# A graph layer on one core: the running maximum written to SBUF, and other shares of the gathers

## The chip, the core and the metric

The kernel runs on one core of a Trainium2 chip. The core has five engines, each with a queue of its own that it works through in order: TensorE (PE; its loads of weights are shown as PEld), VectorE (DVE), ScalarE (ACT), GpSimd (POOL), and SyncE (SP), which here only issues DMAs. They meet at semaphores. SBUF is the working memory of 128 partitions, PSUM the memory of eight banks into which PE writes.

The metric is the time on the device in microseconds, as the median of several runs. A profile is one execution with every instruction recorded.

## The reference

A graph of 12500 nodes and 200000 edges, sorted by destination, goes through a two-layer network; features have 128 elements in fp32. Cut to what matters:

```python
h    = maximum(layernorm(x), 0)
w    = edge_weight / segment_sum(edge_weight, dst)[dst]
feat = relu(h @ W_pool + b_pool)
neigh = segment_max(feat[src] * w, dst)          # layer 1
rst  = h @ W1_self + neigh @ W1_neigh + b1
h    = relu(rst / norm(rst))
neigh2 = segment_sum(h[src] * w, dst) / deg      # layer 2
out  = x + relu(h @ W2_self + neigh2 @ W2_neigh + b2)
```

Each layer fetches one row of 128 features for every edge, by the edge's source, and reduces the rows of the edges that share a destination: by maximum in layer 1, by sum in layer 2. `edge_attr_128` is not used.

## The kernel before

**Tiling.** Edges are taken in groups of G = 512 consecutive ones, 391 groups (the last has 320). A group is four chunks of 128 edges, one edge to a partition. Both layers are one loop over the groups, written out as a software pipeline under `manual_schedule`: what iteration i issues belongs to groups i, i-1, i-2 and so on, and each engine's order is the order in the text.

**Fetching.** A chunk's rows come from a table in HBM (`feat_d`, `h_d`) by an indirect DMA that POOL issues (`gather`, L520), 128 rows each. Some chunks come another way: the node features also lie transposed in SBUF (`one_way`, `other_way`: features by nodes), and VectorE or ACT copies the column of each edge's source out of it (class `Columns`, functions `two_by_two`, L800, two columns an instruction, and `one_by_one`, L788, one an instruction). The column addresses are loaded into registers sixteen at a time from a list in SBUF (`places_of`, L742), which SP loads (`load`, L738), two iterations ahead of the first fetch. `every` says how often an engine takes over a chunk: in layer 1 VectorE takes chunk 1 of each sixth group from group 32 and ACT chunk 3 of each 5.5th; in layer 2 VectorE takes chunk 1 of each third group and ACT chunk 2 of each 3.5th. The fetches of one chunk, eight of sixteen columns, are spread over the iterations before its group; the fetched chunk lies features by edges, so PE must turn it (layer 1 multiplies it by `W_pool`, `multiplied`, L951, and ACT writes it back, `cut`, L954; layer 2 transposes it into the PSUM tile `flip`, `turned`, L1151, and ACT writes it back, `back`).

**Buffers for the rows.** `ring` holds the gathered groups: 18 at first, later 14, and 8 from about group 113 on and in all of layer 2. A gather waits until the group that had its buffer has been used.

**Layer 1, by iteration.** ACT weights the four chunks of group i by the edge weights into `gs` (L1035). PE turns group i-1 into the PSUM tile `pm` (L1040), features by edges. VectorE runs a scan over the 512 edges of group i-2 (L1055): state = max(kept + state, new), where `kept` (`kt`, from `keep_d`) is 0 inside a destination and about -3e38 at its first edge; the scan overwrites `pm` in place, and its last column is the next group's start (`carry`, L1074). No two destinations end within one pair of edges, so 256 values are kept: VectorE copies the odd elements from `pm` to `sc` (L1078), and overwrites an element with its even neighbour where the mask says that a new destination begins at the odd one (`copy_predicated`, L1081). PE turns `sc` back (L1095), ACT copies it to SBUF (L1050), PE multiplies it by a selection matrix built by VectorE (`pick`, L1067; L1104), and ACT writes the 48 columns of the window into the transposed neighbour sums (L985). Whenever the groups of a node tile are done, the node steps (`nodes1`: L851 to L890) run, spread over six iterations; they store the rows of h to `h_d`. `side_step` does background jobs on the edge lists (`edges1` to `fitness`) for layer 2 in between, until 1599 us.

`kt` is loaded by SP for KEPT = 4 groups at a time (`keep_rows`, L602), into one of two buffers, at the start of each fourth iteration.

The first 16 groups (FIRST) go another way: their rows of x are gathered and normalised before the table exists, and the products of rows and weights are made on VectorE (L1084), with the weights in a `gs` tile.

**Layer 2, by iteration.** VectorE makes the weighted places of group i (L1165, L1169), with a fetch between the two; PE multiplies rows and places of group i-1 into a PSUM tile `pa` (`window_product`, L1175, L1177; three buffers); VectorE adds the `pa` of group i-2 to the window of the transposed sums (`window_add`, L1180), after another fetch. The node steps (`nodes2`) run as in layer 1, from iteration 60 on. Three first groups (`early_groups`), gathered before all of `h_d` is written, are put right and added in between.

Of the kernel before, what the change touches and what calls it, by code (L numbers as in the profile page):

```python
# [18 lines left out]
P = 128  # L19
# [22 lines left out]
TABLES_AT = (16512, 66880)  # L42
BURST = 16
HIGH = 1.0e30
KEPT = 4
PAIR = 2


# [1 line left out]
def gnn_kernel(ctx, tc, x, src, dst, ew, w_pool, b_pool, w1s, w1n, b1, w2s, w2n, b2, out):  # L50
# [871 lines left out]
    with tc.manual_schedule(), tc.tile_pool(name="ew", bufs=3) as wk, \  # L922
# [13 lines left out]
        products = {}  # L936
        bycol = []
        for k, engine, copy, j, every, first in (
                (0, mybir.EngineType.DVE, two_by_two, 1, 6, FIRST + 16),
                (1, mybir.EngineType.Activation, one_by_one, 3, 5.5, FIRST + 12)):  # L940

            def rows_of_chunk(g, j=j):
                return buffer(g, True)[:, j, :]

            def slot(g, k=k, rows_of_chunk=rows_of_chunk):
                return rows_of_chunk(g) if k else picked[:, bycol[0].place[g], :]

            def multiplied(g, _, k=k, slot=slot):
                product = products[g, k] = ps.tile([P, D], F32, name="pn")
                nc.tensor.matmul(product, (ones_r if k else minus_plus)[0:3, :P], bias_kept[0:3, :], start=True, stop=False)  # L950
                nc.tensor.matmul(product, slot(g), W["pool"], start=False, stop=True)  # L951

            def cut(g, _, k=k, rows_of_chunk=rows_of_chunk):
                nc.scalar.activation(rows_of_chunk(g), products.pop((g, k)), AF.Relu,  # L954
                                     **({} if k else {"scale": signs}))
# [7 lines left out]
        def keep_tile():  # L963
            return wk.tile([P, KEPT, G], BF16, name="kt", bufs=2)

# [36 lines left out]
        for i in range(max(turn) + 6):  # L1002
# [6 lines left out]
            if i >= NG:  # L1009
                window_copy(due(5))  # L1010
            node_stage(5)
            if i % KEPT == 0 and i and i + 2 < NG:
                keep_rows(i + 2, keep_tile())
            if FIRST <= i < NG:
                gts[i] = gather(buffer(i, True), feat_d, i, besides=bycol)

            if i < FIRST:
                pms[i] = ps.tile([P, G], F32, name="pm", bufs=2)
                if i > 0:
                    nc.scalar.activation(pms[i], raws.pop(i).rearrange("p q n -> p (q n)"), AF.Relu, bias=bp_col)  # L1020
                if i + 1 < FIRST:
                    weight_rows(i + 1, wk.tile([P, G], F32, name="gs", bufs=2))
                    raw_columns(pn, i + 1)
                if i + 2 < FIRST:
                    raw_scale(i + 2)
                    raw_norm(i + 2)
                if i + 1 < FIRST:
                    raw_back(i + 1)

            elif i < NG:  # L1030
                t, r, ne, chunks = edges_of(i)
                gss[i] = wk.tile([P, G], F32, name="gs", bufs=2).rearrange("p (q d) -> p q d", d=D)
                gt = gts.pop(i)
                for j, k in reversed(chunks):
                    nc.scalar.activation(gss[i][:k, j, :], gt[:k, j, :], AF.Copy, scale=ewT[:k, t, j, r:r + 1])  # L1035
            if FIRST < i <= NG:
                gs = gss.pop(i - 1)
                pms[i - 1] = ps.tile([P, G], F32, name="pm", bufs=2)
                for j, k in edges_of(i - 1)[3]:
                    nc.tensor.transpose(pms[i - 1][:, j * P:j * P + k], gs[:k, j, :], ident[:k, :k])  # L1040
# [11 lines left out]
            if g is not None:  # L1052
                ne = edges_of(g)[2]
                kt, pm = kts.pop(g), pms.pop(g)
                nc.vector.tensor_tensor_scan(pm[:, :ne], kt[:, :ne], pm[:, :ne], carry,  # L1055
                                             op0=OP.add, op1=OP.max)
                bycol[0].ahead()
            picks = []
# [12 lines left out]
            if g is not None:  # L1071
                if g + 1 < NG:
                    carry = wk.tile([P, 1], F32, name="carry")
                    nc.vector.tensor_copy(carry, pm[:, ne - 1:ne])  # L1074
                sc = scs[g] = wk.tile([P, G // 2], F32, name="sc", bufs=2)
                two = pm[:, :ne].rearrange("p (c two) -> p c two", two=2)
                new = kt[:, :ne].bitcast(I16).rearrange("p (c two) -> p c two", two=2)
                nc.vector.tensor_copy(sc[:, :ne // 2], two[:, :, 1])  # L1078
            pick()
            if g is not None:  # L1080
                nc.vector.copy_predicated(sc[:, :ne // 2], new[:, :, 1], two[:, :, 0])  # L1081
            if i < FIRST:
                rows = gts.pop(i).rearrange("p q n -> p (q n)")
                nc.vector.tensor_tensor(pms[i], pms[i] if i else rows, ws.pop(i), OP.mult)  # L1084
            node_stage(1)
            node_stage(3)
            node_stage(4)
# [34 lines left out]
                c.turn(i, c.load, c.fetch)  # L1122
            for c in bycol:
                c.turn(i, c.multiplied)
        assert not busy
        i = NG
        side_step()
# [4 lines left out]
    with tc.manual_schedule(), tc.tile_pool(name="ew2", bufs=3) as wk, \  # L1132
            tc.tile_pool(name="ep2", bufs=2, space=PSUM) as ps:
        place = ps.tile([P, 2 * Q, CW], F32, bufs=1)
        hit, iota = place[:, :Q, :], place[:, Q:, :]
        flip = ps.tile([P, 2, P], F32, bufs=1)
        for j in range(Q):
            nc.vector.tensor_copy(iota[:, j, :], cols[:, 0, SHIFT[j]:SHIFT[j] + CW])
        nothing = wk.tile([P, LW], BF16, bufs=1)
# [2 lines left out]
        bycol = []  # L1142
        for k, engine, copy, j, every, first in (
                (0, mybir.EngineType.DVE, two_by_two, 1, 3, 17),
                (1, mybir.EngineType.Activation, one_by_one, 2, 3.5, 12)):

            def slot(g, j=j):
                return buffer(g, False)[:, j, :]

            def turned(g, _, k=k, slot=slot):  # L1150
                nc.tensor.transpose(flip[:, k], slot(g), ident)  # L1151

            def back(g, _, k=k, slot=slot):
                by_scalar(slot(g), flip[:, k], **({} if k else {"scale": signs}))

            bycol.append(Columns(engine, copy, None, other_way, 1, lists_of(k), slot,
                                 ((-2, turned), (0, back)), 3, j, every, first, NG - 1))
            bycol[k].turned, bycol[k].back = turned, back
# [57 lines left out]
        for i in range(max(turn) + 2):  # L1216
# [22 lines left out]
                next(first_groups, None)  # L1239
            if i == NG - 1:  # L1240
                for n in (HI - 2, HI - 1):
                    own[n] = flip[:, 0] if n % 2 else ps.tile([P, Q, D], F32, name="pl", bufs=1)[:, 0]
                    linear_own(own[n], n, "2s")
            by_two, by_one = bycol
            by_two.fetch_one(i)
# [133 lines left out]
```

## Time and profile before

| | us |
|---|---|
| time, median of 3 runs | 3544.11 (3543.92 to 3545.5) |
| the profiled execution's own time | 3545.64 |
| its span, from first to last instruction | 3543.9 |
| DVE busy | 3130.4 (88%) |
| ACT busy | 3081.4 (87%) |
| POOL busy | 2619.8 (74%) |
| PE busy | 2211.6 (62%) |

Layer 1's gathers of `feat_d` end at 1838.4 us; those of `h_d` for the first groups follow. The page gives busy times by engine; groups of instructions by source line, with the mean time of one and the idle time in front of them, by what ended it; the waits list who waited for whom; the timeline lists instructions with start and length; and the windows give busy times and counts of a stretch of time. "issue" is idle time for which the profile shows no wait; loads of registers fall under it, as they are not counted as busy.

### The profile page before, as it was taken

To read this page: it belongs to the slowest core of one execution; us is meant where nothing else is said; L and a number is where in the kernel's file an instruction comes from. 1 tells how busy PE (TensorE), PEld (TensorE's weight loads), DVE (VectorE), ACT (ScalarE), POOL (GpSimd) and SP (SyncE) were. 2 spreads that over 40 slices of the span, in tenths; PEclk is the share of its full clock that TensorE was granted. 3 is DMA by queue.
4 is the path that set the end of the run, shared out by engine and by line. 5 is a ranking of instruction groups with operands and counts; after the bars stand their busy time and mean duration, and the time that the engine had idled before them with its cause. 6 is when DMAs were issued, how large, how long until landed. Compare 5 with 4: busy or idle time off the path is not lost.

```text
span 3543.9 us, 71968 instructions
## 1 busy us (share of the span) xinstructions
PE 2211.6 (62%) x9504; PEld 1920.0 (54%) x9504; DVE 3130.4 (88%) x16737; ACT 3081.4 (87%) x25633; POOL 2619.8 (74%) x2784
## 2 busy tenths in 40 slices
PE   7666666666666666566565667565565556556556
PEld 6455555555656555555554555555455555455545
DVE  7799999999999999998866888888888888888887
ACT  6689999999999999898967888888888888888885
POOL 6577777777777777777777777777777777777774
PEclk8665555555555555555555555555555555555555
DMA  6433332333333333332222222222222222222221
GB/s 223 130 97 90 94 88 83 88 86 88 86 87 86 88 86 88 86 88 86 83 82 54 54 60 75 60 63 63 60 60 63 63 60 62 63 59 59 62 62 49
DMA packets 132987, 280.13 MB, mean 79 GB/s; under 512 B 49446, under 2 KB 58764, under 8 KB 132494
## 3 DMA queue, kind: packets, MB, share of 16 engines
q0 software_dynamic: 88544, 181.42, 20.2%
q1 hardware_dynamic: 43214, 93.11, 7.8%
q14 instruction: 414, 3.39, 0.3%
q8 instruction: 79, 1.29, 0.2%
q10 hardware_dynamic: 736, 0.92, 0.1%
HBM read 253.41 MB, written 21.87 MB: 78 GB/s over the span
## 4 chain that ended last, share of the span: by engine, by line
DVE 49%; ACT 16%; issue 12%; POOL 6%; PE 6%; DVEq 5%; DMA 4%; ACTq 1%; POOLq 0%
DVE gt L800 25%; ACT gt L788 7%; POOL gt L520 6%; DVE pm L1055 6%; DVE picked L800 5%; DVEq L742 5%; ACT gs L1035 4%; DMA gt<-feat_d,srcT 3%; PE pa L1177 2%; DVE sel L1067 2%; DVE s L1169 2%; PE pf L625 2%; DVE sc L1078 2%; DVE place L1165 1%; ACT rows L1050 1%
## 5 line engine op out<-in xcount | busy, mean ns | idle before, releaser
L788 ACT ACTIVATE gt<-way 128x1 f32 x21376 | 2125.3, 189 | 226.8 <-PE pa L1177 164.5
L520 POOL DMA_INDIRECT gt<-h_d,srcT x1318 | 1246.1, 945 | 411.5 <-issue 340.8
L520 POOL DMA_INDIRECT gt<-feat_d,srcT x1192 | 1127.5, 946 | 369.2 <-issue 302.0
L800 DVE SCALAR_TENSOR_TENSOR gt<-b,way 128x2 f32<-128x2 f32 x8000 | 1155.1, 215 | 182.7 <-issue 154.3
L1177 PE MATMUL pa<-s,gt 128*128 128x24 f32 x3102 | 736.5, 390 | 535.0 <-DVE s L1169 462.4
L1177 PEld LDWEIGHTS pa<-s,gt 128*128 128x128 f32 x3102 | 690.6, 327 | 573.4 <-DVE s L1169 502.8
L1040 PE MATMUL pm<-ident,gs 128*128 128x128 f32 x1499 | 393.5, 415 | 257.9 <-ACT gs L1035 232.1
L800 DVE SCALAR_TENSOR_TENSOR picked<-b,way 128x2 f32<-128x2 f32 x3840 | 541.7, 211 | 1.9 <-issue 1.7
L1055 DVE TENSOR_TENSOR_SCAN pm<-kt,carry,pm 128x512 f32<-128x512 bf16 x389 | 496.3, 1276 | 46.0 <-PE pm L1040 45.8
L1035 ACT ACTIVATE gs<-gt,ewT 128x128 f32<-128x128 f32 x1303 | 414.9, 390 | 73.6 <-DMA gt<-feat_d,srcT 60.1
L1104 PEld LDWEIGHTS pn<-sel,rows 128*128 128x128 f32 x1564 | 354.3, 313 | 170.5 <-ACT way L985 73.2
L1040 PEld LDWEIGHTS pm<-ident,gs 128*128 128x128 f32 x1499 | 283.9, 221 | 294.3 <-ACT gs L1035 276.6
L1104 PE MATMUL pn<-sel,rows 128*128 128x48 f32 x1564 | 356.9, 374 | 135.1 <-ACT way L985 58.6
L1067 DVE TENSOR_SCALAR sel<-cols,lastT,invT 128x48 f32<-128x48 f32 x782 | 245.7, 314 | 0.0
L1095 PE MATMUL pr<-ident,sc 128*128 128x128 f32 x782 | 235.9, 403 | 3.4 <-DVE r_first L291 2.4
L1081 DVE COPY_PREDICATED sc<-kt,pm 128x256 f32<-128x256 int16 x389 | 167.1, 430 | 0.0
L1095 PEld LDWEIGHTS pr<-ident,sc 128*128 128x128 f32 x782 | 164.5, 220 | 4.2 <-ACT gs L1035 3.7
L1078 DVE COPY sc<-pm 128x256 f32<-128x256 f32 x391 | 159.7, 408 | 3.8 <-PE pr L1095 3.7
L1050 ACT ACTIVATE rows<-pr 128x256 f32<-128x256 f32 x392 | 142.1, 363 | 5.3 <-PE pn L1104 5.2
L851 PE MATMUL pn<-w_2n,way 128*128 128x128 f32 x192 | 79.2, 515 | 102.2 <-DVE way L1180 102.2
L1165 DVE TENSOR_TENSOR place<-place,locT 128x96 f32<-128x96 f32 x391 | 100.8, 258 | 46.1 <-DVE way L1180 32.2
L520 POOL DMA_INDIRECT w2T<-feat_d,srcT x96 | 90.8, 946 | 51.9 <-issue 24.1
(303 smaller groups left out, 2735.1 us busy)
## 6 DMA issues: line engine op xcount, KB each, us to landing
kt<-keep_d SPq DMA_DIRECT2D x97, 512.0 KB
gt<-h_d,srcT POOLq DMA_INDIRECT x1318
gt<-feat_d,srcT POOLq DMA_INDIRECT x1192
feat_d<-fr SPq DMA_DIRECT2D x24, 256.0 KB
xr<-in_x SPq DMA_DIRECT2D x24, 256.0 KB
out<-o SPq DMA_DIRECT2D x24, 256.0 KB
h_d<-h SPq DMA_DIRECT2D x47, 128.0 KB
listed<-at_d SPq DMA_DIRECT2D x359, 0.5 KB
```

The costliest lines, as they stand in the source:

```text
L520: nc.gpsimd.indirect_dma_start(out=gt[:k, j, :], out_offset=None, in_=table_d[:, :], in_offset=bass.IndirectOffsetOnAxis(ap=srcT[:k, t, j, ...
L788: nc.scalar.activation(out, in_, AF.Copy, **scale)
L800: nc.vector.scalar_tensor_tensor(slot[:, r + e:r + e + 2], zero_high, columns_read[e], columns_read[e + 1].to_broadcast([P, 2]), op0=OP.su ...
L1035: nc.scalar.activation(gss[i][:k, j, :], gt[:k, j, :], AF.Copy, scale=ewT[:k, t, j, r:r + 1])
L1040: nc.tensor.transpose(pms[i - 1][:, j * P:j * P + k], gs[:k, j, :], ident[:k, :k])
L1050: nc.scalar.activation(rws[g][:k, j, :], pr[:k, j, :], AF.Copy)
L1055: nc.vector.tensor_tensor_scan(pm[:, :ne], kt[:, :ne], pm[:, :ne], carry, op0=OP.add, op1=OP.max)
L1067: nc.vector.tensor_scalar(part, cols[:k, 1, :], lastT[:k, t, j, r:r + 1], invT[:k, t, j, r:r + 1], op0=OP.is_equal, op1=OP.mult)
L1078: nc.vector.tensor_copy(sc[:, :ne // 2], two[:, :, 1])
L1095: nc.tensor.transpose(prs[g][:k, j, :], sc[:, j * P:j * P + k], ident)
L1104: nc.tensor.matmul(pas[g], rows[:k, j, :], sel[:k, j, :], start=j == 0, stop=j == len(chunks) - 1)
L1177: nc.tensor.matmul(pas[g][:, SHIFT[j]:SHIFT[j] + CW], gt[:k, j, :], s[:k, j, :], start=False, stop=j == 0)
```

## The change

In layer 1:

- The scan of a group from 16 on writes its result not into `pm` but into the group's weighted rows `gs` in SBUF, which PE has read by then. `carry` is read from there. The copy of the odd elements into `sc` is gone for these groups: `copy_predicated` changes the odd elements in place, reading the even ones from the same tile, and PE turns the odd elements, every second word, out of that tile. `gs` has four buffers, `sc` is gone; the first 16 groups put their copy into a `gs` tile.
- VectorE takes over chunk 1 of each 5.5th group, where it was each sixth.
- `kt` is loaded for three groups at a time, and at the end of the iteration, after the list loads.
- For the first 16 groups the product of rows and weights comes ahead of the copy.

In layer 2:

- The turned tiles lie in two PSUM tiles of a bank each, where they shared one; PE turns a chunk (`turned`) ahead of ACT's fetch and of the copies back in the order of the text. For the bank, `pa` has two buffers, where it had three.
- ACT takes over chunk 2 of each 3.25th group, where it was each 3.5th.

```diff
-KEPT = 4
+KEPT = 3
...
-                (0, mybir.EngineType.DVE, two_by_two, 1, 6, FIRST + 16),
+                (0, mybir.EngineType.DVE, two_by_two, 1, 5.5, FIRST + 16),
...
-            if i % KEPT == 0 and i and i + 2 < NG:
-                keep_rows(i + 2, keep_tile())
...
-                gss[i] = wk.tile([P, G], F32, name="gs", bufs=2).rearrange("p (q d) -> p q d", d=D)
+                gss[i] = wk.tile([P, G], F32, name="gs", bufs=4).rearrange("p (q d) -> p q d", d=D)
...
-                gs = gss.pop(i - 1)
+                gs = gss[i - 1]
...
-                nc.vector.tensor_tensor_scan(pm[:, :ne], kt[:, :ne], pm[:, :ne], carry,
+                most = gss.pop(g).rearrange("p q d -> p (q d)") if g >= FIRST else pm
+                nc.vector.tensor_tensor_scan(most[:, :ne], kt[:, :ne], pm[:, :ne], carry,
                                              op0=OP.add, op1=OP.max)
...
-                    nc.vector.tensor_copy(carry, pm[:, ne - 1:ne])
-                sc = scs[g] = wk.tile([P, G // 2], F32, name="sc", bufs=2)
-                two = pm[:, :ne].rearrange("p (c two) -> p c two", two=2)
-                new = kt[:, :ne].bitcast(I16).rearrange("p (c two) -> p c two", two=2)
-                nc.vector.tensor_copy(sc[:, :ne // 2], two[:, :, 1])
-            pick()
-            if g is not None:
-                nc.vector.copy_predicated(sc[:, :ne // 2], new[:, :, 1], two[:, :, 0])
+                    nc.vector.tensor_copy(carry, most[:, ne - 1:ne])
             if i < FIRST:
                 rows = gts.pop(i).rearrange("p q n -> p (q n)")
                 nc.vector.tensor_tensor(pms[i], pms[i] if i else rows, ws.pop(i), OP.mult)
+            if g is not None:
+                two = most[:, :ne].rearrange("p (c two) -> p c two", two=2)
+                new = kt[:, :ne].bitcast(I16).rearrange("p (c two) -> p c two", two=2)
+                scs[g] = two[:, :, 1]
+                if g < FIRST:
+                    scs[g] = wk.tile([P, G], F32, name="gs", bufs=4)[:, :ne // 2]
+                    nc.vector.tensor_copy(scs[g], two[:, :, 1])
+            pick()
+            if g is not None:
+                nc.vector.copy_predicated(scs[g], new[:, :, 1], two[:, :, 0])
...
             for c in bycol:
                 c.turn(i, c.multiplied)
+            if i % KEPT == 0 and i and i + 2 < NG:
+                keep_rows(i + 2, keep_tile())
...
-        flip = ps.tile([P, 2, P], F32, bufs=1)
+        flips = [ps.tile([P, P], F32, name=f"flip{k}", bufs=1) for k in range(2)]
...
-                (1, mybir.EngineType.Activation, one_by_one, 2, 3.5, 12)):
+                (1, mybir.EngineType.Activation, one_by_one, 2, 3.25, 12)):
...
-                nc.tensor.transpose(flip[:, k], slot(g), ident)
+                nc.tensor.transpose(flips[k], slot(g), ident)
...
-                by_scalar(slot(g), flip[:, k], **({} if k else {"scale": signs}))
+                by_scalar(slot(g), flips[k], **({} if k else {"scale": signs}))
...
-            pas[g] = ps.tile([P, LW], F32, name="pa", bufs=3)
+            pas[g] = ps.tile([P, LW], F32, name="pa", bufs=2)
...
             by_two.turn(i, by_two.fetch)
+            for c in bycol:
+                c.turn(i, c.turned)
             by_one.fetch_one(i)
             for c in bycol:
                 c.turn(i, c.back)
-            for c in bycol:
-                c.turn(i, c.turned)
```

More of the change, by code (lines that the diff above doesn't have):

```diff
@@ L1021, in gnn_kernel @@
                 if i + 1 < FIRST:
-                    weight_rows(i + 1, wk.tile([P, G], F32, name="gs", bufs=2))
+                    weight_rows(i + 1, wk.tile([P, G], F32, name="gs", bufs=4))
                     raw_columns(pn, i + 1)
@@ L1241, in gnn_kernel @@
                 for n in (HI - 2, HI - 1):
-                    own[n] = flip[:, 0] if n % 2 else ps.tile([P, Q, D], F32, name="pl", bufs=1)[:, 0]
+                    own[n] = flips[0] if n % 2 else ps.tile([P, Q, D], F32, name="pl", bufs=1)[:, 0]
                     linear_own(own[n], n, "2s")
```

## The prediction

> **What bounds the kernel now.** The page first: three engines are close to full, so shares over the whole span cannot say which one sets the end.
>
> ```profile
> span 3543.9 us, 71968 instructions
> PE 2211.6 (62%) x9504; PEld 1920.0 (54%) x9504; DVE 3130.4 (88%) x16737; ACT 3081.4 (87%) x25633; POOL 2619.8 (74%) x2784
> ```
>
> Next the busy times in three stretches: layer 1 in its first two thirds, its last third, and the middle of layer 2. The columns are stretch, length, then PE, PEld, DVE, ACT, POOL, each with its count.
>
> ```profile
> 300.00:1300.00 1000.00, 639.18 (x2911) 569.10 (x2911) 978.62 (x4178) 956.75 (x7062) 751.70 (x796) 0.55 0.31 88
> 1300.00:1800.00 500.00, 307.63 (x1354) 273.21 (x1353) 459.07 (x2019) 447.77 (x3342) 378.24 (x399) 0.53 0.31 86
> 2200.00:3400.00 1200.00, 708.26 (x2946) 610.09 (x2946) 1016.19 (x6903) 1044.73 (x10353) 902.86 (x956) 0.50 0.24 61
> ```
>
> Then the gathers themselves in time, here in layer 2, and the step from layer 1 to layer 2:
>
> ```profile
> 3479.55 0.95 POOL L520 DMA_INDIRECT gt<-h_d,srcT  x1 [0.30 <-issue]
> 3480.80 1.04 POOL L520 DMA_INDIRECT gt<-h_d,srcT  x1 [0.30 <-issue]
> 3482.15 0.94 POOL L520 DMA_INDIRECT gt<-h_d,srcT  x1 [0.31 <-issue]
> ...
> 1837.52 0.91 POOL L520 DMA_INDIRECT gt<-feat_d,srcT  x1 [0.30 <-issue]
> 1841.94 1.03 POOL L520 DMA_INDIRECT er<-h_d,srcT  x1 [3.51 <-DVE sc L1081]
> ```
>
> A gather costs POOL 0.95 us and 0.30 us before the next one, 1.25 us in all. In 1300 to 1800 us POOL issues 399 of them, 1.253 us each: its 76% busy is a full queue. Who waits for it is in the waits, first of POOL (300 to 1300 us), then of ACT (1300 to 1800 us):
>
> ```profile
> POOL gt L520 <- ACT rows L1050: 7.5, 5, 4.3
> ...
> ACT gs L1035 <- DMA gt<-feat_d,srcT: 40.5, 26, 4.5
> ```
>
> In all of layer 1's middle POOL loses 7.5 - 5 x 0.30 = 6.0 us (longest 4.3, near 600 us, where the ring of gather buffers has shrunk to eight groups); after 1300 us ACT waits for gathers that are late. So layer 1 ends when POOL has issued its gathers, although VectorE is 98% busy in the first stretch: there VectorE and ACT work off a backlog, and POOL does not wait for it except for those 6 us.
>
> Layer 2 is different. The window additions (L1180, one per group) in its middle, and the waits there of POOL, DVE and ACT:
>
> ```profile
> 2200.00:3400.00 1200.00, 54.91 (x279) 0.50 0.24 61
> ```
> ```profile
> POOL gt L520 <- PE pa L1177: 28.3, 74, 2.8
> ...
> DVE gt L800 <- issue: 118.5, 410, 1.3
> DVE way L1180 <- PE pa L1177: 0.2, 1, 0.2
> ...
> ACT gt L788 <- PE pa L1177: 104.0, 46, 6.3
> ACT gt L788 <- issue: 29.0, 84, 0.8
> ACT gt L788 <- PE flip L1151: 16.2, 12, 3.1
> ```
>
> A group takes 1200 / 279 = 4.30 us, while POOL needs (4 - 1/3 - 1/3.5) x 1.25 = 4.23 us for its gathers. VectorE waits for no other engine (0.2 us); its idle time is "issue", the loads of column addresses. POOL and ACT wait for PE, which waits for VectorE. So VectorE paces layer 2, POOL is just behind it.
>
> **The change part by part.** These rows price it (groups by shape, and a stretch of VectorE's time order):
>
> ```profile
> L788 ACT ACTIVATE gt<-way 128x1 f32 x21376 | 2125.3, 189 | 226.8 <-PE pa L1177 164.5 <-issue 53.1 <-DMA gt<-h_d,srcT 1.5
> L800 DVE SCALAR_TENSOR_TENSOR picked<-b,way 128x2 f32<-128x2 f32 x3840 | 541.7, 211 | 1.9 <-issue 1.7
> L1055 DVE TENSOR_TENSOR_SCAN pm<-kt,carry,pm 128x512 f32<-128x512 bf16 x388 | 495.4, 1277 | 45.5 <-PE pm L1040 45.3
> L414 DVE TENSOR_TENSOR_SCAN r_f<-r_goes,r_first,pq 128x512 f32<-128x512 bf16 x4 | 5.1, 1272 | 0.2 <-ACT pq L281 0.2
> ```
> ```profile
> 1204.70 0.41 DVE L1078 COPY sc<-pm 128x256 f32<-128x256 f32 x1
> 1205.04 0.29 DVE L1067 TENSOR_SCALAR sel<-cols,lastT,invT 128x48 f32<-128x48 f32 x1
> 1205.25 0.43 DVE L1081 COPY_PREDICATED sc<-kt,pm 128x256 f32<-128x256 int16 x1
> 1205.58 1.13 DVE L800 SCALAR_TENSOR_TENSOR picked<-b,way 128x2 f32<-128x2 f32 x8
> ```
>
> *Six gathers fewer in layer 1.* VectorE's share goes from 3840 / 64 = 60 chunks to 66 (from group 32, each 5.5th, below 390). POOL: 6 x 1.25 = -7.5 us, all of it on the path that ends layer 1. The six products on PE and their cuts on ACT (about 0.4 us each) go into idle time.
>
> *VectorE in layer 1.* The copy of the odd elements (L1078) falls away for groups 16 and up: start to start 0.34 us x 375 = -127 us. Six more chunks cost 6 x 541.7 / 60 = +54 us. With 5.5 every second chunk's address list is loaded only in the iteration in which the chunk before is finished, so its first addresses are no longer read ahead: 33 x up to 1.3 us (the longest issue wait above), +43 us, at least 0. The scan writes SBUF: L414 does that at 1272 ns against 1277, so 0. Net -30 to -73 us, about 2 to 4% of layer 1. It is not on the path: it lets the backlog shrink earlier, so of POOL's 6.0 us I take 3.5 as saved (bounds 0 and 6.0), since ACT, 96% busy beside it, gains nothing and limits the gain.
>
> *The predicated copy with both inputs in SBUF.* Here the change touches POOL. Before, its data came from PSUM, its mask from SBUF. How POOL fares beside the two kinds:
>
> ```profile
> 3480.74 0.29 DVE L911 SCALAR_TENSOR_TENSOR o<-o,xr 128x128 f32<-128x128 f32 x1
> ...
> 1156.38 0.43 DVE L1081 COPY_PREDICATED sc<-kt,pm 128x256 f32<-128x256 int16 x1
> ...
> 1156.50 0.94 POOL L520 DMA_INDIRECT gt<-feat_d,srcT  x1 [0.30 <-issue]
> ```
>
> L911 adds two SBUF tensors; the gather that started 0.06 us after it took 1.04 us instead of 0.94 or 0.95. The predicated copy of before started 0.12 us ahead of a gather that took 0.94 us. So a gather needs something, early in its run, that an operation with two SBUF inputs holds. [...] The price: 128 elements held a gather up 0.10 us; 128 more at about 1 us per 1000 elements (L1201 less L865, 384 elements more in 691 - 277 ns) make 0.24 us for 256.
>
> ```profile
> L865 DVE TENSOR_TENSOR r<-pn,b 128x128 f32<-128x128 f32 x96 | 26.6, 277 | 4.3 <-PE pn L851 4.3
> L1201 DVE TENSOR_TENSOR er<-pl,er 128x512 f32<-128x512 f32 x3 | 2.1, 691 | 0.7 <-issue 0.4 <-DMA gt<-h_d,srcT 0.3
> ```
>
> If it falls anywhere in POOL's 1.25 us, one in 1.25 / 0.24 = 5.2 hits a gather's start and delays it by half of 0.24: 0.024 us a copy, x 375 = +9 us of POOL, on the path. Bounds: 0 (not held) and the second rival's 36. I take +9.
>
> *Stride.* The copy now reads and writes every second word in SBUF. ScalarE writes with the same stride of two (L890) against none (L954), and with four (L621) against none (L559):
>
> ```profile
> L890 ACT ACTIVATE way<-pn 128x128 f32<-128x128 f32 x98 | 27.5, 281 | 7.4 <-issue 2.8 <-PE pn L888 2.3 <-PE pr L1095 1.9
> L954 ACT ACTIVATE gt<-pn 128x128 f32<-128x128 f32 x59 | 15.9, 270 | 4.3 <-PE pn L951 4.3
> ...
> L559 ACT ACTIVATE gt<-pn 128x512 f32<-128x512 f32 x7 | 4.0, 578 | 0.0
> L621 ACT ACTIVATE way<-pt 128x512 f32<-128x512 f32 x24 | 25.7, 1073 | 23.3 <-PE pt L637 23.3
> ```
>
> Stride two costs 11 ns over 128 elements, stride four 495 ns over 512, 0.97 ns each. The first has the very stride, so I take 0.02 us for 256; the second, 0.25 us, is the upper end.
>
> *Buffers and queues in layer 1.* Four weighted-row buffers instead of two: ACT's write of group i now waits for PE's turn of group i-4 after the predicated copy of VectorE's iteration i-2; before it waited, through the scan's buffer, for that same copy. Nothing. PE's scan buffer is free after the scan instead of four operations later, a small relief. The kept rows load 130 times instead of 98, at the iteration's end, behind the node stores and list loads on SP; their wait, for the copy of the same iteration, is over when VectorE has gone on, and the rows are wanted three iterations (13 us) later. POOL's queue is not passed. The tail of layer 1 loses one copy: -0.3 us.
>
> *Layer 2.* VectorE's instructions stay the same, so its pace does. ACT fetches 117 chunks instead of 108 and POOL issues nine gathers less, -11 us: hidden, for POOL waits for VectorE already; without that cover it would be a gain of 11. ACT's load in the 1200 us grows by 1/13 of 80 chunks, 6 x 128 x 2125.3 / 21376 us = 78 us, against 104.0 + 16.2 = 120 us that it waits now; what goes is the wait for PE, and next late are its address loads (29.0 us), which fit. Two product buffers instead of three: PE's product of group i-1 waits for the addition of group i-3 instead of the weights of i-1, later in VectorE's iteration i-1 by one fetch of sixteen columns (1.13 us in the row above) and the addition. Behind it wait the turned tiles, ACT's next fetch and POOL's ring; VectorE wants the product in iteration i+1, more than one group (4.3 us) after its end. Turned tiles in two banks and issued ahead of the copies back take a wait from ACT (16.2 us) that VectorE never sees. I take 0 (bounds -11 and +25, below).
>
> **Sum.** -7.5 - 3.5 + 9 - 0.3 + 0 = -2.3 us. The profiled execution took 3545.64 us (span 3543.9 and 1.7 around it), so it would take 3543.3; it stands 1.5 above the median of 3544.11, and against the median the forecast is 3542 us. Within 0.2% (7 us) of the median I call it the same, about what a measurement of this kernel can tell from no change.
>
> **Rivals.** *POOL is not held up* (faster): the predicated copy may read its mask in another way than L911 its second tensor. Then -11.3, 3533 us. For it: the 3840 two-element operations read two SBUF tensors too, and the 399 gathers beside them took 378.24 / 399 = 0.95 us each; against it: they are over in 0.14 us, and the 1.04 us above.
>
> *Stride two is dear* (slower): with L621's price the copy takes 0.25 us more and holds 0.49 us: 0.49 x 0.49 / 2.5 x 375 = +36 us for POOL in place of +9, and VectorE gets 93 us more, which undoes its relief, so the 3.5 us aren't saved: -7.5 + 36 - 0.3 = +28, 3572 us. It decides once the copy runs over about 0.55 us. [...]
>
> *ACT becomes layer 2's bound* (slower): if half of its 120 us of waits stay, because a slot is released later by two product buffers, 78 us don't fit into 60: 18 us per 1200, 25 us over layer 2, 3568 us. Against it: the fetch of a chunk has some four groups' time.
>
> *Layer 2 follows POOL after all* (faster): 11 us more, 3532 us; VectorE's missing waits speak against it.
>
> **How the numbers follow.** Forecast 0.44, of which 0.04 ends below and 0.05 above the same; not held 0.20, stride 0.14, ACT 0.13, POOL 0.09. Faster 0.04 + 0.20 + 0.07 = 0.31, slower 0.05 + 0.14 + 0.11 = 0.30, same the rest, 0.39. The range runs from the faster rivals (3533, and some us for the error of their terms) to ACT's (3568), with part of the stride case left out above it; the likeliest case's own range is 3536 to 3550.
>
> **What would show it.** In the profile after: no L1078 beyond 16; gathers of layer 1 beside the predicated copy at 1.0 to 1.2 us now and then, else 0.94; the copy near 0.43 us or less; layer 1's last gather within 3 us of 1837.5; L1180 still at 279 per 1200 us; ACT near 93% in layer 2 with little wait for PE. A copy above 0.55 us, a window of layer 2 with other than 277 to 281 additions, or gathers all at 0.94 us make it wrong.

## The result and the profile after

The changed kernel takes 3573.31 us (median of 4 runs, 3569.79 to 3574.05) beside 3544.34 us for the kernel before, in the same comparison: a ratio of 1.0078, with a 95% interval of 1.0065 to 1.0090. It is 29 us slower; the forecast was 3542 us, the same within 0.2%. The profiled execution took 3573.47 us. Its page, with span and busy times:

```profile
span 3571.7 us, 73511 instructions
PE 2233.4 (63%) x9531; PEld 1934.5 (54%) x9531; DVE 3145.0 (88%) x16746; ACT 3194.0 (89%) x26800; POOL 2632.9 (74%) x2769
```

The busy shares say little: ACT's has risen by two points, the others by one or none. The stretches and the turn from one layer to the other say where it happened. The same three windows as before, then the window additions of layer 2 (now L1184), and POOL's time order around the end of layer 1:

```profile
300.00:1300.00 1000.00, 642.04 (x2874) 566.13 (x2874) 970.99 (x4096) 938.58 (x6910) 753.00 (x780) 0.55 0.29 86
1300.00:1800.00 500.00, 316.48 (x1344) 278.84 (x1345) 463.20 (x2017) 447.18 (x3336) 380.23 (x394) 0.50 0.28 85
2200.00:3400.00 1200.00, 707.36 (x2960) 612.71 (x2960) 1015.26 (x6909) 1119.96 (x11144) 894.92 (x948) 0.50 0.21 61
```
```profile
2200.00:3400.00 1200.00, 54.97 (x279) 0.50 0.21 61
```
```profile
1861.42 0.90 POOL L520 DMA_INDIRECT gt<-feat_d,srcT  x1 [0.30 <-issue]
1868.78 1.03 POOL L520 DMA_INDIRECT er<-h_d,srcT  x1 [6.46 <-DVE r L865]
...
1884.46 0.96 POOL L520 DMA_INDIRECT gt<-h_d,srcT  x1 [0.30 <-issue]
```

Layer 2 makes 279 additions in 1200 us, as before. Layer 1's last gather ends at 1862.3 instead of 1838.4 us: 24 of the 28 us of span are there. And yet POOL was busier, with fewer gathers: 394 in 500 us took 380.23 us, 0.965 us each, where 399 took 378.24. The groups by shape name both causes. First the gathers and the predicated copy in the kernel before, then four groups of the changed kernel:

```profile
L520 POOL DMA_INDIRECT gt<-feat_d,srcT x1192 | 1127.5, 946 | 369.2 <-issue 302.0 <-ACT gs L1035 22.6 <-DMA gt<-feat_d,srcT 11.9
L1081 DVE COPY_PREDICATED sc<-kt,pm 128x256 f32<-128x256 int16 x388 | 166.8, 430 | 0.0
```
```profile
L520 POOL DMA_INDIRECT gt<-feat_d,srcT x1187 | 1146.4, 966 | 371.3 <-issue 273.0 <-DMA gt<-feat_d,srcT 42.4 <-ACT gs L1033 23.8
L800 DVE SCALAR_TENSOR_TENSOR picked<-b,way 128x2 f32<-128x2 f32 x4224 | 593.0, 212 | 22.8 <-issue 22.3
L1054 DVE TENSOR_TENSOR_SCAN gs<-kt,carry,pm 128x512 f32<-128x512 bf16 x374 | 473.9, 1267 | 27.8 <-PE pm L1038 19.7 <-issue 3.9 <-ACT way L985 2.1
L1086 DVE COPY_PREDICATED gs<-kt,gs 128x256 f32<-128x256 int16 x374 | 269.5, 721 | 0.4
```

The predicated copy takes 721 ns where it took 430, and the mean gather of layer 1 966 ns where it took 946 (layer 2's are at 945 in both). How the two belong together is seen in the time order, VectorE's row first, then POOL's, at two copies:

```profile
1225.65 0.71 DVE L1086 COPY_PREDICATED gs<-kt,gs 128x256 f32<-128x256 int16 x1
...
1241.18 0.72 DVE L1086 COPY_PREDICATED gs<-kt,gs 128x256 f32<-128x256 int16 x1
1241.70 1.25 DVE L1054 TENSOR_TENSOR_SCAN gs<-kt,carry,pm 128x512 f32<-128x512 bf16 x1
```
```profile
1225.71 1.27 POOL L520 DMA_INDIRECT gt<-feat_d,srcT  x1 [0.30 <-ACT gt L954]
...
1241.04 0.94 POOL L520 DMA_INDIRECT gt<-feat_d,srcT  x1 [0.30 <-DMA gt<-feat_d,srcT]
```

The gather that starts 0.06 us after a copy is done 0.33 us late; one that had started 0.14 us before the copy runs its 0.94 us. Over the whole of layer 1 a gather is held up when a copy starts between some 0.35 us before it (few start earlier than 0.25) and 0.1 us after it: about 126 of the 374 copies did that, for 0.24 us each. The copies that hold a gather up are no longer than the others (0.72 us both), so it is POOL alone that waits. The copy's last rows also show that VectorE's next operation starts 0.52 us after the copy's start, not 0.72: the end of the copy overlaps with what follows, as it did before (0.33 of 0.43 us).

**The account of the 28 us.** "Held" is the sum over layer 1's gathers of their length less 0.946 us; "stalls" are POOL's gaps of over 0.36 us among them, less 0.305 each; the last columns are the end of the last gather of `feat_d`, the time from there to the first of layer 2's regular gathers, and from that one to the end of the span. In runs in which nothing holds gathers up, their mean lies between 0.9445 and 0.9464 us, so "held" is known to about 2 us.

| kernel | gathers | mean, us | held, us | stalls, us | last one ends | to layer 2 | layer 2 |
|---|---|---|---|---|---|---|---|
| before | 1373 | 0.946 | 0 | 6.0 | 1838.4 | 19.6 | 1685.8 |
| after | 1367 | 0.966 | 27.7 | 9.6 | 1862.3 | 22.1 | 1687.2 |

Six gathers fewer -7.5, held +27.7, stalls +3.6, the turn to layer 2 +2.5, layer 2 +1.4: 27.7 of the 27.8 us by which the span grew.

**What of it was on the path.** The sum hides that POOL was held up in two places that count differently. 7.2 of the 27.7 us fall ahead of the stall near 600 us, where POOL waits for a buffer of the full ring anyway. These are the gathers that end the stall: in the kernel before, in the changed kernel, and in a run below (`psum_data`) in which no gather is held up and the copy is as slow:

```profile
604.67 0.94 POOL L520 DMA_INDIRECT gt<-feat_d,srcT  x1 [4.28 <-ACT rows L1050]
613.54 0.94 POOL L520 DMA_INDIRECT gt<-feat_d,srcT  x1 [8.36 <-ACT rows L1048]
614.11 0.94 POOL L520 DMA_INDIRECT gt<-feat_d,srcT  x1 [15.05 <-ACT rows L1048]
```

So up to there the changed kernel loses 8.9 us because the buffer comes later, whether gathers are held up or not; after it 20.6 us of holds, less 5.0 for four of the six saved gathers and 0.5 for short stalls, make up the rest of the 24 us. The hold-up is worth about 20 us, not 28.

### The profile page after: what moved, and what is told of

It is laid out like the page before. It is cut to its first block, busy times and chain, and to the rows that moved or that the text cites. A ratio compares the mean times of both kernels' runs of the same rounds, so it can differ in the third digit from the quotient of the medians.

```text
span 3571.7 us, 73511 instructions
## 1 busy us (share of the span) xinstructions
PE 2233.4 (63%) x9531; PEld 1934.5 (54%) x9531; DVE 3145.0 (88%) x16746; ACT 3194.0 (89%) x26800; POOL 2632.9 (74%) x2769
## 4 chain that ended last, share of the span: by engine, by line
DVE 37%; issue 10%; ACT 6%; DMA 5%; POOL 5%; DVEq 5%; PE 2%; ACTq 0%; POOLq 0%
DVE gt L800 27%; POOL gt L520 5%; DVEq L742 5%; DMA gt<-feat_d,srcT 4%; ACT gt L788 3%; ACT gs L1033 2%; DVE s L1173 2%; DVE picked L800 2%; DVE gs L1054 1%; DVE place L1169 1%; DVE way L1184 1%; DMA gt<-h_d,srcT 1%; DVE o L910 1%; PE pa L1181 1%; DVE sel L1066 1%
## 5 line engine op out<-in xcount | busy, mean ns | idle before, releaser
L788 ACT ACTIVATE gt<-way 128x1 f32 x22528 | 2239.2, 189 | 151.4 <-PE pa L1181 96.1
L520 POOL DMA_INDIRECT gt<-feat_d,srcT x1187 | 1146.4, 966 | 371.3 <-issue 273.0
L800 DVE SCALAR_TENSOR_TENSOR picked<-b,way 128x2 f32<-128x2 f32 x4224 | 593.0, 212 | 22.8 <-issue 22.3
L1054 DVE TENSOR_TENSOR_SCAN gs<-kt,carry,pm 128x512 f32<-128x512 bf16 x375 | 474.8, 1266 | 27.8 <-PE pm L1038 19.7
L1179 PE MATMUL pa<-nothing,ones_r 1*128 1x48 bf16 x391 | 78.6, 201 | 529.4 <-DVE way L1184 528.0
L1086 DVE COPY_PREDICATED gs<-kt,gs 128x256 f32<-128x256 int16 x375 | 270.0, 720 | 0.4
L1097 PE MATMUL pr<-ident,gs 128*128 128x128 f32 x782 | 240.3, 409 | 4.1 <-DVE b L808 2.1
L1066 DVE TENSOR_SCALAR sel<-cols,lastT,invT 128x48 f32<-128x48 f32 x782 | 228.1, 317 | 0.3 <-issue 0.3
L1097 PEld LDWEIGHTS pr<-ident,gs 128*128 128x128 f32 x782 | 167.5, 226 | 8.1 <-issue 3.2
```

What stands on the lines that cost most here:

```text
L520: nc.gpsimd.indirect_dma_start(out=gt[:k, j, :], out_offset=None, in_=table_d[:, :], in_offset=bass.IndirectOffsetOnAxis(ap=srcT[:k, t, j, ...
L788: nc.scalar.activation(out, in_, AF.Copy, **scale)
L800: nc.vector.scalar_tensor_tensor(slot[:, r + e:r + e + 2], zero_high, columns_read[e], columns_read[e + 1].to_broadcast([P, 2]), op0=OP.su ...
L1054: nc.vector.tensor_tensor_scan(most[:, :ne], kt[:, :ne], pm[:, :ne], carry, op0=OP.add, op1=OP.max)
L1066: nc.vector.tensor_scalar(part, cols[:k, 1, :], lastT[:k, t, j, r:r + 1], invT[:k, t, j, r:r + 1], op0=OP.is_equal, op1=OP.mult)
L1086: nc.vector.copy_predicated(scs[g], new[:, :, 1], two[:, :, 0])
```

## The experiments

The account says where, but not what makes the copy slow, what holds POOL up, and whether the parts of the change add up. Theory A (after the result): a step of two words on the copy's output makes it slow; its two SBUF inputs hold gathers up, the longer the copy the more; layer 2 is neutral because VectorE paces it. Against it stand four others: the inputs make the copy slow, whatever the step; the long copy itself holds POOL up, whatever its inputs; the larger share of VectorE does the harm; or layer 2 carries part of it.

**Layer 2's part alone** (the kernel before with the layer 2 hunks of the diff).

> The kernel before with only layer 2's part of the change: turned tiles in two banks and issued ahead of the copies back, two product buffers instead of three, ScalarE's share each 3.25th group. If layer 2 is paced by VectorE as before: no change, 3541 to 3547 us, 279 window additions in 1200 us of its middle. If layer 2 carries part of the 29 us: 3550 us or more. If it follows POOL: 3533 us.

3547.49 us, ratio 1.0007 (0.9997 to 1.0017); the middle of layer 2:

```profile
2200.00:3400.00 1200.00, 705.57 (x2955) 611.45 (x2954) 1015.72 (x6907) 1120.34 (x11127) 895.70 (x948) 0.50 0.23 61
```

POOL has 948 gathers left there instead of 956, ACT is 93% busy instead of 87%, and layer 2 takes 1687.5 us instead of 1685.8. The time is 0.5 us above its 3541 to 3547 us, its interval takes in no change, and the middle has 279 additions: the part is worth nothing, as forecast, and the loss is layer 1's.

**The two halves of layer 1's part.** First the scan and the copy in SBUF without VectorE's larger share (the changed kernel), then that share alone (the kernel before):

```diff
-                (0, mybir.EngineType.DVE, two_by_two, 1, 5.5, FIRST + 16),
+                (0, mybir.EngineType.DVE, two_by_two, 1, 6, FIRST + 16),
```

> The changed kernel with VectorE's share of layer 1 left at each 6th group. Theory hold-up on POOL: 374 copies of 0.72 us hold gathers up by 0.074 us each, 28 us, and no gather is saved; VectorE gains 127 and loses 108 us, so the stall near 600 us stays at 4 to 7 us: 3568 to 3576 us, layer 1's last gather near 1866 us. Theory that the share of each 5.5th group does most of the harm (alone it cost 15 us): 3555 to 3560 us, last gather below 1855 us.

```diff
-                (0, mybir.EngineType.DVE, two_by_two, 1, 6, FIRST + 16),
+                (0, mybir.EngineType.DVE, two_by_two, 1, 5.5, FIRST + 16),
```

> The kernel before with only VectorE's share of layer 1 raised to each 5.5th group. Theory that POOL's gathers alone end layer 1: six gathers fewer, 7.5 us less, 3536 to 3539 us. Theory that VectorE's backlog decides: VectorE gets 54 to 97 us more, its lag behind POOL, 6 us from group 300 on in the kernel before, stays at 20 to 60 us to the end of layer 1, the stall of the gather ring near 600 us grows, 3555 to 3590 us.

The first takes 3575.90 us, ratio 1.0086 (1.0069 to 1.0103): held 33.7 us, stalls 0 (4 to 7 were expected; POOL, held up by 9.1 us by then, now comes to the ring after the buffer), last gather at 1866.2 us, where 1838.4 + 33.7 - 6.0 makes 1866.1. So the copy in SBUF alone costs as much as the whole change; that the larger share adds or saves anything on top of it isn't shown (1.0078 with it, 1.0086 without, and the intervals overlap). Alone, however, that share takes 3560.14 us, ratio 1.0042 (1.0025 to 1.0059), though it too saves six gathers. The two losses don't add up: both fall on the same stall, which ends at 614.8 us with the share alone and at 613.5 us with the whole change. POOL's waits in 300 to 1300 us show how:

```profile
POOL gt L520 <- ACT rows L1050: 22.2, 8, 18.8
POOL gt L520 <- ACT gs L1035: 18.0, 54, 1.6
```

The stall near 600 us grows from 4.3 to 18.8 us, and VectorE, 487.58 us busy in 1300 to 1800 us instead of 459.07, still starts the scan of group 361 24.9 us after that group's last gather (6.9 in the kernel before), so that layer 2 starts 27.4 us after layer 1's last gather instead of 19.6. From 300 to 1840 us VectorE's waits for other engines fall from 63 to 2.4 us: its room was some 60 us wide, and this share uses it up.

**What makes the copy slow, and what holds POOL up.** Three variants of the changed kernel, which leave out the right choice of elements as their expectations say. Adjacent words on both sides:

```diff
+                if g >= FIRST:
+                    two = most[:, :ne].rearrange("p (two c) -> p c two", two=2)
                 scs[g] = two[:, :, 1]
```

> The changed kernel, but the predicated copy takes the first half of the scanned row into the second half (256 adjacent words each) instead of the even into the odd words; both inputs stay in SBUF. It leaves out the right choice of elements, the amount of work is the same. Theory stride (a step of two words in SBUF makes the copy slow, and a long copy with two SBUF inputs holds gathers up): copy back at 0.43 us or less, layer 1's gathers at a mean of 0.950 to 0.957 us instead of 0.966, 3545 to 3556 us. Theory inputs (the copy is slow because both inputs come from SBUF, whatever the step): copy still 0.72 us, gathers 0.966 us, 3573 us.

The output alone in adjacent words:

```diff
-                scs[g] = two[:, :, 1]
-                if g < FIRST:
-                    scs[g] = wk.tile([P, G], F32, name="gs", bufs=4)[:, :ne // 2]
+                scs[g] = wk.tile([P, G // 2], F32, name="sc", bufs=2)[:, :ne // 2]
+                if g < FIRST + 2:
                     nc.vector.tensor_copy(scs[g], two[:, :, 1])
```

> The changed kernel with the predicated copy's output in a buffer of its own, in adjacent words; the data still come from the scanned row in SBUF with a step of two (three buffers of rows instead of four). The odd elements are left out from the third group of the scan on. Theory that the step of the output alone makes the copy slow: 0.43 to 0.45 us, gathers of layer 1 at a mean of 0.955 to 0.959 us, 3550 to 3560 us, as with the dense copy. Theory that the step of the data in SBUF does it: 0.70 us or more, 0.966 us, 3568 to 3576 us. Each its half: 0.55 to 0.60 us, about 3563 us.

The scan's result and so the data in PSUM, as in the kernel before, the output with its step of two in SBUF:

```diff
-                most = gss.pop(g).rearrange("p q d -> p (q d)") if g >= FIRST else pm
+                most = pm
+                rows_in = gss.pop(g).rearrange("p q d -> p (q d)") if g >= FIRST else pm
...
-                scs[g] = two[:, :, 1]
+                scs[g] = rows_in[:, :ne].rearrange("p (c two) -> p c two", two=2)[:, :, 1]
```

> The changed kernel, but the scan writes to PSUM as in the kernel before and the predicated copy takes its data from there, into the odd words of the weighted rows in SBUF; only the mask is an SBUF input. The scanned odd elements are left out. Theory hold-up by two SBUF inputs: no gather of layer 1 is held up (mean 0.946 us), about 28 us less, 3539 to 3547 us, even if the copy stays long. Theory that the long copy itself or its writes with a step of two hold gathers up: mean 0.966 us, 3570 us. The copy's time tells the step of the output alone: 0.43 us if the output's step costs nothing, 0.72 us if it is all of it.

The copy and layer 1's gathers among the groups by shape, in this order:

```profile
L1088 DVE COPY_PREDICATED gs<-kt,gs 128x256 f32<-128x256 int16 x374 | 163.1, 436 | 0.3
L520 POOL DMA_INDIRECT gt<-feat_d,srcT x1187 | 1135.8, 957 | 369.7 <-issue 291.0 <-ACT gs L1033 28.4 <-DMA gt<-feat_d,srcT 12.5
```
```profile
L1085 DVE COPY_PREDICATED sc<-kt,gs 128x256 f32<-128x256 int16 x374 | 163.4, 437 | 0.7 <-PE pr L1096 0.7
L520 POOL DMA_INDIRECT gt<-feat_d,srcT x1187 | 1133.8, 955 | 370.9 <-issue 296.2 <-ACT gs L1033 26.2 <-DMA gt<-feat_d,srcT 13.4
```
```profile
L1087 DVE COPY_PREDICATED gs<-kt,pm 128x256 f32<-128x256 int16 x388 | 272.8, 703 | 0.0
L520 POOL DMA_INDIRECT gt<-feat_d,srcT x1187 | 1122.7, 946 | 378.0 <-issue 295.9 <-ACT gs L1033 28.0 <-ACT rows L1048 17.2
```

| kernel | output | data | copy, us | held, us | stalls, us | time, us | ratio (95%) |
|---|---|---|---|---|---|---|---|
| after | SBUF, step 2 | SBUF, step 2 | 0.721 | 27.7 | 9.6 | 3573.31 | 1.0078 (1.0065 to 1.0090) |
| dense | SBUF, adjacent | SBUF, adjacent | 0.436 | 14.9 | 8.0 | 3558.00 | 1.0041 (1.0027 to 1.0055) |
| out_dense | SBUF, adjacent | SBUF, step 2 | 0.437 | 13.0 | 9.2 | 3558.14 | 1.0035 (1.0021 to 1.0049) |
| psum_data | SBUF, step 2 | PSUM, step 2 | 0.703 | 0 | 16.3 | 3550.65 | 1.0015 (1.0005 to 1.0024) |

The two effects come apart cleanly. The step of the output makes the copy slow, with data from SBUF or PSUM alike (0.721 and 0.703 us); the step of the data costs nothing (0.437 against 0.436). The kernel before is the fourth case: data from PSUM with the step, output adjacent, 0.430 us. That the changed copy works within one tile is not it either, for the dense copy does so too (0.436 us). "Held" and "stalls" are of the profiled executions; that of `dense` was the fastest of five (3552.27, the others 3555.64 to 3562.35), and its median is 2 us above the range expected. And in these runs POOL is held up only when both inputs, mask and data, lie in SBUF (13.0 to 27.7 us): a copy of 0.70 us with data from PSUM holds no gather up (mean 0.946 us). The last time is above its 3539 to 3547 us, because the ring's stall grew to 16.3 us: VectorE is as late there as in the changed kernel (the scan of group 112 starts 10.8 us later than before, in the changed kernel 10.7), and POOL, not held up, waits the longer for the same buffer.

**How the hold grows.** The adjacent copy, cut to half its length:

```diff
-                nc.vector.copy_predicated(scs[g], new[:, :, 1], two[:, :, 0])
+                some = ne // 4 if g >= FIRST else ne // 2
+                nc.vector.copy_predicated(scs[g][:, :some], new[:, :some, 1], two[:, :some, 0])
```

> The changed kernel with the copy of adjacent words cut to its first 128 of 256 elements (it leaves out the other half and the right choice of elements). The copy of 256 held up about 3 in 10 gathers' starts by 0.15 us each, 15 us in all. Theory that the hold grows with the copy's length: a copy of 0.29 to 0.31 us, a third to a half of the gathers held as before, 0.05 to 0.1 us each, 3 to 8 us in all, mean of layer 1's gathers 0.948 to 0.952 us. Theory that each copy with two SBUF inputs costs POOL a fixed time: 13 to 16 us in all, 0.956 us.

```profile
L1089 DVE COPY_PREDICATED gs<-kt,gs 128x128 f32<-128x128 int16 x374 | 110.8, 296 | 0.0
L520 POOL DMA_INDIRECT gt<-feat_d,srcT x1187 | 1126.6, 949 | 373.1 <-issue 289.8 <-ACT gs L1033 28.1 <-DMA gt<-feat_d,srcT 18.0
```

Held 3.8 us in all, with a copy of 0.296 us (3551.52 us in one run). A fixed time for each copy is thereby excluded; with 14.9 us at 0.436 the hold grows with the copy's length, and faster than it, as a window that takes in more gathers and delays each of them longer must. The scan, which writes to SBUF in this run too, can have no more than these 3.8 us, give or take the 2 above. By the prediction's formula (window squared over 2.5, times 374) the windows are 0.16, 0.32 and, for the copy of 0.721 us, 0.43 us. The last step is too small for the length alone: gathers that start up to 0.09 us after the copy are held 0.11, 0.22 and 0.34 us with the three copies (0 with data from PSUM), so 0.14 us more of an adjacent copy hold them 0.11 us longer, and 0.285 us more that come from the output's step only 0.12. Why is open.

**Layer 2, with VectorE relieved.** If layer 2 is paced by VectorE and POOL comes next, fewer chunks for VectorE must make it faster, and the nine gathers that ACT takes off POOL must count from there on. The kernel before with layer 2's part of the change and

```diff
-                (0, mybir.EngineType.DVE, two_by_two, 1, 3, 17),
+                (0, mybir.EngineType.DVE, two_by_two, 1, 3.25, 17),
```

> The kernel before with layer 2's part of the change, and VectorE's share of layer 2 from each 3rd to each 3.25th group: ten chunks and about 92 us less for VectorE, ten gathers more for POOL than with the share of each 3rd, 1319 in all. Theory that VectorE paces layer 2 and POOL comes right behind: POOL sets 1319 x 1.25 = 1649 us and a tail of 15 to 29 us, 1664 to 1678 us in place of 1686, so 3523 to 3537 us; 283 to 284 window additions in 1200 us. Theory that ScalarE, 93% busy with each 3.25th, is the bound by now, or that layer 2 waits for something else: 3543 us or more, 279 additions.

and the same with 3.5:

> As the run with each 3.25th group, but each 3.5th: eighteen chunks less for VectorE, 1327 gathers. By POOL's pace: 1327 x 1.25 = 1659 us and a tail of 15 to 20 us, 1674 to 1679 us in layer 2, 3532 to 3538 us, some 8 us above the run with each 3.25th. If VectorE paced layer 2 still: faster than with each 3.25th, 3525 us or less.

3522.72 us, ratio 0.9935 (0.9918 to 0.9951), and 3529.91 us, ratio 0.9955 (0.9939 to 0.9972); layer 2 takes 1663.6 and 1671.3 us, with 1319 and 1327 gathers. The windows of the first in the middle of layer 2, and the waits there, of DVE and of POOL:

```profile
2200.00:3400.00 1200.00, 700.62 (x3013) 616.85 (x3012) 970.86 (x6574) 1140.17 (x11346) 907.52 (x960) 0.50 0.24 62
```
```profile
DVE gt L800 <- issue: 98.5, 305, 1.0
DVE gt L800 <- PE pa L1177: 63.9, 49, 3.1
...
POOL gt L520 <- issue: 225.2, 739, 0.3
POOL gt L520 <- PE pa L1175: 27.4, 90, 0.3
```

Now VectorE's fetches wait 63.9 us for PE's products, which they did not in this stretch of the kernel before; no wait of POOL in these rows is longer than its own 0.3 us between two gathers (2.8 before), and 960 in 1200 us are its pace of 1.25 us. Both times came out below what was expected, by 0.3 us (3523 to 3537) and by 2.1 us (3532 to 3538). Two more runs tell the rest: VectorE at 3.25 alone, without the change's part (ACT at 3.5, 1328 gathers), and VectorE at 3.125 with it (1314).

> VectorE's share of layer 2 at each 3.25th group alone, for a comparison beside a kernel before of about 3545 us. Expected as before: 3532 to 3536 us if POOL sets layer 2 once VectorE has room and nine gathers are worth 11 us; 3520 to 3525 us if the change's part of layer 2 has no worth even then.

> VectorE's share of layer 2 at each 3.125th group with the change's part of layer 2, for a comparison beside a kernel before of about 3545 us. Expected as before: 3515 to 3519 us if POOL still sets the pace; 3524 to 3535 us if VectorE's pace takes over again.

3533.19 us, ratio 0.9962 (0.9948 to 0.9976), and 3515.24 us, ratio 0.9912 (0.9896 to 0.9929). So layer 2's part, worth nothing in the change, is worth about 10 us (3533.2 less 3522.7, from two comparisons; 11 foretold for its nine gathers) once VectorE has room. What its other pieces, the order and the buffers, have of this was not separated. The five gathers that 3.125 saves over 3.25 give another 7.5. At 3.125 VectorE has only 9.0 us of waits for products left, so this is near where its pace takes over again. That kernel, layer 1 of before and layer 2 of the change with VectorE at each 3.125th group, beats both kernels, by 31 us and by 58.

**Two attempts that tell nothing.** The last two kernels had been run twice before, beside a kernel before that itself took 5108 and 5115 us there.

> The kernel before with VectorE's share of layer 2 at each 3.25th group and nothing else (ScalarE's share stays at each 3.5th, turned tiles in one bank): 1328 gathers of layer 2, nine more than the run that also has the change's part of layer 2 (3522.7 us). If POOL sets layer 2 once VectorE has room, those nine are worth 9 x 1.25 = 11 us: 3532 to 3536 us. If the change's part of layer 2 has no worth even then: 3520 to 3525 us.

> As the run with each 3.25th group of VectorE and the change's part of layer 2, but each 3.125th: 120 chunks for VectorE, 1314 gathers, five fewer. If POOL still sets the pace: 6 us less, 3515 to 3519 us. If VectorE's pace takes over again: 3524 to 3535 us.

> The same kernel as in the first run of this edit, beside which the kernel before took 5108 us, with ScalarE's address loads as the bound; taken again for a comparison in which the kernel before takes about 3545 us. Expected as before: 3532 to 3536 us if POOL sets layer 2 once VectorE has room and the nine gathers are worth 11 us; 3520 to 3525 us if the change's part of layer 2 has no worth even then.

> The same kernel as in the first run of this edit, taken again beside a kernel before of about 3545 us. Expected as before: 3515 to 3519 us if POOL still sets the pace with VectorE's share at each 3.125th group; 3524 to 3535 us if VectorE's pace takes over again.

They took 5138.83 and 5226.19, then 5136.66 and 5215.05 us. ACT's column copies take their usual 190 ns, but ACT waits before them for nothing that the profile shows (over the whole span, first run):

```profile
L788 ACT ACTIVATE gt<-way 128x1 f32 x21376 | 2365.7, 190 | 1458.8 <-issue 1412.6 <-PE pa L1177 26.6 <-remote 2.1
```

In the kernel before's own profile that wait is 53.1 us. The kernel with more fetches for ACT is the slower one here. Why ACT waits is open; no conclusion is drawn from these four runs.

## Why the prediction was wrong

- *What bounds the kernel.* Right in the main. Layer 1's gathers ended 24 us later, and in layer 2 POOL had room that VectorE's pace hid, as the runs with a smaller share of VectorE show.
- *Stride.* **This is the step that failed.** The prediction priced the copy too low, and the hold and VectorE's load hang on that price. It took ScalarE's step of two (11 ns over 128 elements) for VectorE's and put the copy at +0.02 us; it is +0.29 us, just above the upper end of 0.25. The choice between two ends far apart went by the row with the same step but another engine. VectorE itself pays less than the length says: start to start the copy costs it 0.19 us more (0.52 instead of 0.33). The second rival had this right for the output: from L621's price it put the copy at +0.25 us. For the input it doesn't hold here: data with a step of two cost 437 ns against 436.
- *Both inputs in SBUF.* The mechanism was right as far as the rows told it: with both inputs in SBUF gathers are held up (0.946 us before, 0.957 in `dense`, 0.966 after), with the data from PSUM they are not (0.946 us in `psum_data`); what it is that a gather needs there, no run shows. That a hold grows by all of a copy's extra length, as the second rival had it, is not borne out: the slow copy's extra 0.285 us lengthen a hold by 0.12. The size was wrong too: at 0.436 us the copy holds up 14.9 us instead of 9, since by the formula the window is 0.32 us wide and not 0.24; at 0.721 us it is 27.7, of which about 20 cost time.
- *Six gathers fewer.* -7.5 us, right, but the term of 3.5 us saved at the ring's stall had the wrong sign: +3.6. VectorE's net relief of 30 to 73 us became a load of about 45. Along its time order in layer 1, from start to start, the predicated copy adds 76 us, the chunks 53, the address lists 25 and smaller operations 17, against 126 saved. Even with the short copies the stall is 8 to 11 us. Part of that is simple: two of the six saved gathers lie ahead of it, so POOL comes to the ring 2.5 us earlier. The buffer itself comes 4 to 5 us later there than before (608.5 to 609.6 us instead of 604.7). VectorE waits longer for ACT in these runs (`ss`, L872, in 120 to 600 us: 10.1 us in the run with the half copy, 1.4 before), and what share of the stall that has was not separated.
- *Layer 2.* 0, measured +1.4 us, and for the reason given: from 2200 to 3400 us PE waits 426.6 us for the addition, where it waited 393.6 for the weighted places, and VectorE waits for PE's products 0.2 us, as before.
- In the forecast's own sum the hold is +27.7 in place of +9, the stall +3.6 in place of -3.5, the turn to layer 2 +2.5 in place of -0.3, and layer 2 +1.4 in place of 0. The second rival as a whole gave 3572 us, within 2 us, with a chance of 0.14. Its mechanism was the right one, its number partly luck: a hold 8 us too dear (36) made up for a stall and a turn to layer 2 that it had not foreseen. The time lies 5 us above 3568, the upper end of the range, which left part of this rival out.

## What to carry to other kernels

Ask of each VectorE operation that is moved into SBUF two things before its count of instructions: does its output keep adjacent words (here the copy took 0.436 us with them, 0.721 with a step of two), and does it now have two SBUF inputs beside a GpSimd queue that is the bound (here gathers were held up by 14.9 and 27.7 us in all). Here an operand in PSUM cost nothing (0.430 us before, 0.436 for the adjacent copy in SBUF) and left GpSimd free (0 us held with the data from PSUM), so saving a copy was dearer than the copy. And where one engine's relief is worth nothing, look who paces the stage: relieved there, the same part of the change was worth about 10 us. Ask too where the waiting queue stands still anyway: what held it up ahead of such a stall, 7.2 of 27.7 us here, cost nothing.

## What the runs showed that was not expected

- The predicated copy on VectorE, writing every second word of SBUF, costs by estimate 2.2 ns an element here, against 1.09 with adjacent words (from 296 ns for 128 and 436 for 256: 156 ns fixed; 721 for 256 with the step, if its fixed part is the same); reading every second word of the data cost nothing (437 ns against 436).
- The hold-up is one-sided in these runs: the copy delays a gather (by 0.24 us on average where it takes 0.721 us) only if it starts up to about 0.1 us after it, or before it by no more than some 0.15, 0.25 and 0.35 us for copies of 0.296, 0.436 and 0.721 us. A gather further under way neither waits nor lengthens the copy (0.72 us all the same).
